# Two attention layers on one core: early queries with half the keys, and a new written order

## The chip, the cores and the metric

The kernel runs on one core of a Trainium2 chip. The metric is the device time of one execution in microseconds (us). A core has a matrix engine (TensorE, here PE; its weight loads are listed apart as PEld), a vector engine (VectorE, DVE), a scalar engine (ScalarE, ACT), a general engine (GpSimd, POOL) and a sync engine (SyncE, SP), which here only issues DMAs. Each engine works through its own queue in order and waits for others by semaphores. SBUF is the working memory with 128 partitions, PSUM the memory that PE writes.

## The reference, cut to what matters

There are 64 items of 128 positions with 512 features, and two attention layers one after the other. Both have 16 heads of 64 features, one key and one value shared by all heads, and one learned "null" key and value ahead of the 128 others. Each layer adds its normalised output to x.

```python
# one layer; q has 16 heads, k and v one
sim = einsum('bhid,bjd->bhij', q, k) + bias      # layer 1: * 8, q and k normalised
sim = where(causal, neg, sim)                    # key j hidden from query i if j > i
sim = where(mask, sim, neg)                      # padding of each item
attn = softmax(sim)                              # over the null key and 128 keys
out = einsum('bhij,bjd->bhid', attn, v)
return layernorm(out.reshape(b, n, 1024) @ Wo)
```

Layer 0 takes its bias from an input. Layer 1 makes it from the distance of two positions by a small network. Because of the causal mask, queries 0 to 63 see no key beyond 63.

## The kernel before, in words

**Tiling.** All of an item's 128 positions lie in the partitions. Matrix products with weights are done in three passes of float32r matmuls (high part by high, high by low, low by high), which `split_lo` (L125) and copies on ACT prepare. Layer 0 handles items in pairs: `Duo.direct` (L412) projects the first 14 heads of two items at once, already transposed; the last two heads come with key, value and null column from `Batch.project` (L535) and are transposed in `query_T` (L661). Layer 1 projects an item by `project` in three banks of 464, 448 and 256 columns (`BANKS`, L31), takes squared norms (`take`, L555; `power`, L581), scales (`scale`, L622) and transposes the queries in three parts.

**Softmax.** Four groups g of four heads follow. `bias_mask` (L683, POOL) adds bias and padding mask into a tile s of 128 x 4 x 129; five such tiles exist. `logits` (L697, PE) makes two pairs of heads: the stationary operand is two heads' transposed queries, the moving one a key tile of 256 columns (`kbh`, `kbl`) that holds the transposed key twice in block form, so one matmul gives two heads. `peak` (L706, DVE) adds and takes the maximum for each head; `exps` (L717, ACT) writes the null column and takes four exponentials with their sums; `recip` (L727, DVE) inverts the sums; `weigh` (L743, POOL) or, in layer 1 for groups 1 and 3, `weigh_scaled` (L734, ACT) multiplies.

**Transposition through DRAM.** `turn` (L753, DVE) transposes 32 x 32 blocks, `send` (L760) writes a group's blocks to DRAM, and `fetch` (L771) reads half an item (two groups h) back with the keys in the partitions, as `pT`. `values` (L778, PE) multiplies it with v in plain float32: two products of 64 output partitions each, side by side in the array. `values_high` (L790, ACT) and `values_low` (L794, DVE) split the result, `output` (L801, PE) does the three passes of the output projection per pair of heads. `out_stats` to `store` (L812 to L829) normalise, add and write.

**Order.** Nothing is scheduled by the compiler on PE, DVE, ACT and POOL: `STEPS` lists each step of a pair (layer 0) or an item (layer 1) with a time in units of `SPAN` (32.5 and 17.0 us), these are repeated for all pairs and items (`at`, L1106), sorted, and each engine's queue is filled in that order. The times are no clocks, only the order counts. SP is not in the list of ordered engines (`ENGINES`, L51). `OUT_STEPS` and `with_room` (L1122) put the preparation of later weights and of layer 1's bias in between; `begin` (L842) does the first pair's start by hand.

Of the kernel before, what the change touches and what calls it, by code (L numbers as in the profile page):

```python
# [28 lines left out]

# [3 lines left out]
    ((0, H + 7 * DH), (H + 7 * DH, 7 * DH), (H + 14 * DH, 4 * DH)),  # L33
# [3 lines left out]
VALC = (17 * DH, H + 7 * DH)  # L37
QHEADS = (((14, 16),), ((0, 6), (6, 12), (12, 16)))
QCOLS = (
    ((0, 16, 0),),  # L40
    ((0, 6, H + DH), (6, 10, H + 8 * DH)),
)
# [12 lines left out]
    mybir.EngineType.Pool,  # L55
}
# [3 lines left out]
def tile_two_attention_layers(ctx: ExitStack, tc: tile.TileContext, a, out: bass.AP):  # L60
# [24 lines left out]
    bias1 = pdr.tile([P, H, S], F32, tag="bias1", name="bias1")  # L85
# [137 lines left out]
    def by_column(t):  # L223

        return t.rearrange("p m (k b) -> p m b k", b=NS)

    def columns(t):
        return t.rearrange("p m (b k) -> p m b k", b=NS)

    def causal(bias, out):  # L230

        nc.gpsimd.affine_select(
            out=bias, in_=bias, compare_op=ALU.is_ge, fill=NEG, base=0,
            pattern=[[0, 4], [-1, S]], channel_multiplier=1,
        )
        nc.scalar.copy(columns(out), by_column(bias))

    def prep_bias1():
# [106 lines left out]
        def rows_of_table():  # L345

            work = p1.tile([P, 2, DIM], F32, tag="work", name="table")
            tb = work[0:H, 0, 0 : 2 * P]
            nc.vector.memset(tb, NEG)
            nc.vector.tensor_scalar_add(tb[:, S - 1 : 2 * S - 1], d["ps"], d["b2"])  # L350
            scratch = pdr.tile([H, 2 * P], F32, tag="scratch", name="scratch")
            nc.sync.dma_start(out=scratch, in_=tb)
            d["raw"] = wts.tile([P, H, S], F32, tag="wh1", name="raw_bias")
            nc.sync.dma_start(
                out=d["raw"],
                in_=bass.AP(scratch.tensor, scratch.offset, [[1, P], [2 * P, H], [1, S]]),
            )
            d["bias"] = wts.tile([P, H, S], F32, tag="wl1", name="bias1")

        def in_order(m):  # L360
            ms = slice(4 * m, 4 * m + 4)
            nc.scalar.copy(columns(d["bias"][:, ms, :]), by_column(d["raw"][:, ms, ::-1]))
            nc.sync.dma_start(out=bias1[:, ms, :], in_=d["bias"][:, ms, :])
# [17 lines left out]
    def mask_rows(L, b):  # L381
        if (L, b // MB) not in mu8s:
            mu8 = mu8s[L, b // MB] = p2.tile([P, MB, S], U8, tag="mu8", name="mu8")
            nc.sync.dma_start(
                out=mu8.rearrange("p b s -> p (b s)"),
                in_=masks[L].rearrange("b s -> (b s)")[b // MB * MB * S : (b // MB + 1) * MB * S]
                .partition_broadcast(P),
            )

    def mask_row(L, b):  # L390
        g = b // MB
        if (L, g) not in madds:
            madd = madds[L, g] = p2.tile([P, MB, S], F32, tag="madd", name="madd")
            nc.gpsimd.tensor_scalar(
                columns(madd), by_column(mu8s[L, g]), -NEG, NEG, ALU.mult, ALU.add
            )
        return madds[L, g][:, b % MB, :]

    class Duo:
# [34 lines left out]

        def direct_high(self, n):
            self.q[n] = [
                p1.tile([P, 2 - n // 3, 2, P], F32R, tag=f"qT{part}{n}", name="qT")
                for part in "hl"
            ]
            nc.scalar.copy(self.q[n][0], self.ps[n])  # L440

        def direct_low(self, n):
            split_lo(self.q[n][1], self.ps[n], self.q[n][0])

    class Batch:


        def __init__(self, L, b, t):
# [6 lines left out]
            self.q, self.qh, self.ql, self.pt_q = {}, {}, {}, {}  # L455
# [79 lines left out]
        def project(self, n, k, steps=None, columns=None):  # L535
# [4 lines left out]
            e = 4 if self.L == 0 else 2  # L540
# [14 lines left out]
        def take(self, n):  # L555
# [4 lines left out]
            if self.L == 0:  # L560
                self.q[n] = p1.tile([P, (h1 - h0) * DH], F32, tag="q0", name="q")
                nc.scalar.copy(self.q[n], ps[:, e : e + 2 * DH])
                return
            if n == 0:
                e = KEYC[1]
                self.rn = p4.tile([P, H + 1], F32, tag="rn", name="rn")
            m = (BANKS[1][n][1] - e) // DH
            rn = self.norms(n)
            for k in range(m):
                sq = p2.tile([P, DH], F32, tag="sq", name="sq")  # L570
                nc.scalar.activation(  # L571
                    sq, ps[:, e + k * DH : e + (k + 1) * DH], AF.Square,
                    accum_out=rn[:, k : k + 1],
# [18 lines left out]
        def value(self):  # L592

            self.v = p4.tile([P, DH], F32, tag="v", name="v")
            nc.vector.tensor_tensor(self.v, self.part(VALC, self.L, DH), nvrow, ALU.subtract)

# [12 lines left out]
        def null(self):  # L609

            self.nln, self.mx, self.den = (
                p4.tile([P, H], F32, tag=name, name=name) for name in ("nln", "mx", "den")
            )
            null = self.part(NULLC, 0, H)
            if self.L == 0:
                nc.vector.scalar_tensor_tensor(  # L616
                    self.nln, null, -1.0, self.w["nbias"], ALU.mult, ALU.subtract
                )
            else:
                nc.vector.tensor_scalar_mul(self.nln, null, -1.0)  # L620

        def scale(self, n):  # L622
# [5 lines left out]
            self.q[n] = p1.tile([P, nh * DH], F32, tag=("q0", "q1", "qTh3")[n], name="q")  # L628
            nc.vector.tensor_tensor(
                self.q[n].rearrange("p (h d) -> p h d", d=DH),  # L630
# [5 lines left out]
        def null_scale(self):  # L636

            nc.vector.tensor_tensor(self.nln, self.nln, self.rn[:, 1:], ALU.mult)  # L638
            nc.vector.tensor_tensor(self.nln, self.nln, self.w["nbias"], ALU.subtract)  # L639
# [4 lines left out]

        def key_high(self):
            self.kh, self.kl = kbh[self.t % NB], kbl[self.t % NB]
            for t in range(2):
                half = slice(t * DH, (t + 1) * DH)
                nc.scalar.copy(
                    columns(self.kh[half, t : t + 1, :]), by_column(self.pk[half, None, :])  # L650
                )

        def key_low(self):
            for t in range(2):
                half = slice(t * DH, (t + 1) * DH)
                split_lo(
                    columns(self.kl[half, t : t + 1, :]), by_column(self.pk[half, None, :]),
                    columns(self.kh[half, t : t + 1, :]),
                )

        def query_T(self, m):  # L661
            n = (QHEADS[self.L][m][1] - QHEADS[self.L][m][0]) // 2
            pt = self.pt_q[m] = ps_tr.tile([P, n, P], F32, tag="tr", name="pt_q")
            for k in range(n):
                nc.tensor.transpose(pt[:, k, :], self.q[m][:, k * P : (k + 1) * P], ident)  # L665

        def query_high(self, m):
            pt = self.pt_q[m]
            tag = f"qTh{m}" if self.L else "q1"
            self.qh[m] = p1.tile(list(pt.shape), F32R, tag=tag, name="qh")  # L670
            nc.scalar.copy(self.qh[m], pt)

        def query_low(self, m):
            pt = self.pt_q[m]
            tag = f"qTl{m}" if self.L else "ql"
            self.ql[m] = p1.tile(list(pt.shape), F32R, tag=tag, name="ql")
            split_lo(self.ql[m], pt, self.qh[m])
# [517 lines left out]
```

## Time and profile before

| what | value |
|---|---|
| time, median of 3 runs | 2434.31 us (2432.69 to 2436.56) |
| the profiled execution's own time | 2435.07 us |
| its span in the trace | 2433.2 us, granted PE clock 0.992 |
| PE busy | 2344.2 us (96%) |
| DVE busy | 2138.1 us (88%) |
| ACT busy | 1784.4 us (73%) |
| POOL busy | 1803.2 us (74%) |
| DMA | 455.72 MB, 62.3% of 16 engines' span |

The span reaches from the first to the last instruction; 1.9 us of the execution lie around it. In the views below, a row names line, engine, operation, what it writes from what it reads (out<-in), shapes and count; "idle" and "waited for" name the engine and line that ended a wait. Records of one engine overlap where its work is pipelined, so the distance of two starts tells more of a price than a record's length. In a timeline row the first column is the start and the second the length, in us.

### The profile page before, as it was taken

To read this page: it belongs to the slowest core of one execution; us is meant where nothing else is said; L and a number is where in the kernel's file an instruction comes from. 1 tells how busy PE (TensorE), PEld (TensorE's weight loads), DVE (VectorE), ACT (ScalarE), POOL (GpSimd) and SP (SyncE) were. 2 spreads that over 40 slices of the span, in tenths; PEclk is the share of its full clock that TensorE was granted. 3 is DMA by queue.
4 is the path that set the end of the run, shared out by engine and by line. 5 is a ranking of instruction groups with operands and counts; after the bars stand their busy time and mean duration, and the time that the engine had idled before them with its cause. 6 is when DMAs were issued, how large, how long until landed. Compare 5 with 4: busy or idle time off the path is not lost. (4 is left out here: it accounts for less than half of the span.)

```text
span 2433.2 us, 50606 instructions
## 1 busy us (share of the span) xinstructions
PE 2344.2 (96%) x13672; PEld 1870.6 (77%) x13672; DVE 2138.1 (88%) x7801; ACT 1784.4 (73%) x8424; POOL 1803.2 (74%) x2015
## 2 busy tenths in 40 slices
PE   5999999999999999999989999999999999999998
PEld 5778777778878878877677777778777777777785
DVE  7988888888888888888899999999999998999997
ACT  4656666656656656556578898899988898898985
POOL 5766677777776676676677888878877887888773
PEclk8999999999999999999999999999999999999999
DMA  5666666666666666666666666666666666666654
GB/s 171 188 175 202 200 198 185 195 207 193 198 202 183 192 192 184 192 191 186 202 188 175 193 180 193 189 182 195 184 188 182 183 190 183 175 192 190 181 170 143
DMA packets 568764, 455.72 MB, mean 187 GB/s; under 512 B 36112, under 2 KB 497952, under 8 KB 568480
## 3 DMA queue, kind: packets, MB, share of 16 engines
q1 hardware_dynamic: 568480, 452.50, 62.3%
q8 instruction: 109, 1.79, 0.3%
q14 instruction: 175, 1.43, 0.2%
HBM read 251.06 MB, written 201.34 MB: 186 GB/s over the span
## 5 line engine op out<-in xcount | busy, mean ns | idle before, releaser
L722 ACT ACTIVATE s<-s,mx 128x129 f32<-128x129 f32 x2048 | 800.4, 393 | 109.0 <-DVE mx L712 85.8
L685 POOL TENSOR_TENSOR s<-bias,madd 128x512 f32<-128x512 f32 x512 | 680.8, 1332 | 84.6 <-DVE den L729 68.2
L712 DVE CUSTOM_DVE_ANT_0 s<-sim,s,nln 128x128 f32<-128x128 f32 x2048 | 587.1, 344 | 1.9 <-PE sim L704 0.9
L747 POOL TENSOR_TENSOR s<-s,den 128x512 f32<-128x512 f32 x384 | 404.4, 1053 | 170.4 <-DVE den L729 102.6
L807 PE MATMUL y<-woh,oh 128*128 128x512 f32 x1024 | 416.3, 407 | 0.1
L807 PE MATMUL y<-wol,oh 128*128 128x512 f32 x1024 | 406.6, 397 | 0.7 <-DVE wol L127 0.7
L807 PE MATMUL y<-woh,ol 128*128 128x512 f32 x1024 | 404.0, 395 | 0.7 <-DVE ol L796 0.7
L755 DVE STREAM_TRANSPOSE tt<-s 128x512 f32<-128x512 f32 x512 | 353.8, 698 | 38.6 <-DMA turned<-tt 33.7
L722 ACT ACTIVATION_READ_ACCUMULATOR s<-s,mx 128x1 f32 x2048 | 382.5, 187 | 0.0
L546 PE MATMUL pq<-wh,xh 128*128 128x272 f32 (+3 forms) x1024 | 348.0, 340 | 2.5 <-DVE nln L638 2.3
L546 PE MATMUL pq<-wh,xl 128*128 128x272 f32 (+3 forms) x1024 | 344.2, 336 | 0.0
L546 PE MATMUL pq<-wl,xh 128*128 128x272 f32 (+3 forms) x1024 | 334.8, 327 | 0.0
L792 ACT ACTIVATE oh<-av,nvcol 128x512 fp32r<-128x512 f32 x256 | 174.8, 683 | 196.6 <-PE av L781 196.5
L781 PE MATMUL av<-pT,v 128*64 128x512 f32 x1024 | 277.5, 621 | 7.5 <-DMA pT<-turned 7.1
L107 POOL TENSOR_TENSOR rn<-rn,neghalf 128x7 f32<-128x7 f32 (+2 forms) x192 | 254.2, 1324 | 16.0
L428 PE MATMUL pqT<-xh,wh 128*128 128x256 f32 x896 | 255.1, 289 | 8.9 <-DVE nln L616 4.1
L428 PE MATMUL pqT<-xh,wl 128*128 128x256 f32 x896 | 253.3, 286 | 4.2 <-DVE wl L182 4.2
L428 PE MATMUL pqT<-xl,wh 128*128 128x256 f32 x896 | 254.3, 286 | 0.0
L571 ACT ACTIVATE sq<-pq 128x64 f32<-128x64 f32 x1088 | 225.6, 227 | 19.1 <-PE pq L546 17.4
L807 PEld LDWEIGHTS y<-woh,oh 128*128 128x128 f32 x1024 | 193.7, 189 | 53.8 <-issue 28.2
L807 PEld LDWEIGHTS y<-woh,ol 128*128 128x128 f32 x1024 | 193.3, 189 | 49.3 <-DVE ol L796 2.2
L546 PEld LDWEIGHTS pq<-wh,xh 128*128 128x128 f32 x1024 | 193.8, 189 | 48.4 <-issue 9.2
(106 smaller groups left out, 5831.9 us busy)
## 6 DMA issues: line engine op xcount, KB each, us to landing
turned<-tt SPq DMA_DIRECT2D x636, 256.0 KB, 3.5
pT<-turned SPq DMA_DIRECT2D x256, 512.0 KB, 4.3
xT<-turned SPq DMA_DIRECT2D x124, 256.0 KB, 3.1
x<-in_x_dram SPq DMA_DIRECT2D x64, 256.0 KB, 3.3
xr<-in_x_dram SPq DMA_DIRECT2D x64, 256.0 KB, 2.9
mid<-xr SPq DMA_DIRECT2D x64, 256.0 KB, 3.4
x<-mid SPq DMA_DIRECT2D x64, 256.0 KB, 3.7
xr<-mid SPq DMA_DIRECT2D x64, 256.0 KB, 2.8
```

The source lines that it names most:

```text
L107: nc.gpsimd.tensor_tensor(t, t, neghalf[:, 0:n], ALU.pow)
L428: nc.tensor.matmul(self.ps[n][:, hp, :, :], lhs[:, c, e : e + P], rhs[:, c, :, :],  start=(i == 0 and (hp == 0 or chunks is None)), stop=( ...
L546: nc.tensor.matmul(self.ps[n][:, c0:c1], lhs[:, c, :], rhs[:, c, n0 + c0 : n0 + c1], start=(i == 0), stop=(i == 3 * NC - 1),)
L571: nc.scalar.activation(sq, ps[:, e + k * DH : e + (k + 1) * DH], AF.Square, accum_out=rn[:, k : k + 1],)
L685: nc.gpsimd.tensor_tensor(s[:, :, 0:S], self.w["bias", g], self.mrow[:, None, :].to_broadcast([P, 4, S]), ALU.add,)
L712: nc.vector.tensor_tensor_reduce(s[:, k, 0:S], self.sim[g][:, k, :], s[:, k, 0:S], -1.0, self.nln[:, h : h + 1], ALU.add, ALU.min, self.mx ...
L722: nc.scalar.activation(s[:, k, :], s[:, k, :], AF.Exp, bias=self.mx[:, h : h + 1], scale=-1.0, accum_out=self.den[:, h : h + 1],)
L747: nc.gpsimd.tensor_tensor(s, s, self.den[:, gs, None].to_broadcast([P, 4, S]), ALU.mult)
L755: nc.vector.transpose(tt.rearrange("p b h i -> p h b i"), self.s[g][:, :, 0:S].rearrange("p h (b k) -> p h b k", k=SQ),)
L781: nc.tensor.matmul(av[t * DH : (t + 1) * DH], self.v, self.pT[h][:, :, t::2, :].rearrange("p i c q -> p c i q"), start=True, stop=True,)
L792: nc.scalar.activation(self.oh[h], self.av[h], AF.Identity, bias=nvcol)
L807: nc.tensor.matmul(self.y, lhs, rhs[:, c, :], start=(c == 0 and k == 0), stop=(c == NP - 1 and k == 2),)
```

## The change

The 64 early queries (f = 0) and the 64 late ones (f = 1) get tiles of their own. A query tile now has, in its 128 partitions after the logits, 64 queries of one head (m = 0) and the same 64 queries of another (m = 1); a group's row is 2 heads (t) by 64 + 128 keys (`KC` = 192), with a null column at each end: 2 x 194 in place of 4 x 129. The transposed query tiles are laid out accordingly.

- `logits`: per group three matmuls with 128 columns (early, 64 keys of two heads) and three with 256 (late), where six had 256.
- `peak`, `exps`, `weigh_scaled`: two operations over 64 keys and two over 128 where four had 128; `bias_mask`, `weigh` and `turn` 384 columns for 512; `recip` two instructions for one, because the late reciprocal is written twice for the broadcast.
- `null` and `null_scale` place the null columns by four operations on 64 partitions; `value` writes a second tile `ve`, the first 64 keys' values in the upper partitions.
- `send` once for half an item (384 KB) in place of twice (256 KB); `fetch` three transfers of 128 KB into `pTe`, the early tile that both halves share, and `pT`. Two of the `tt` tiles exist as before, now larger.
- `values(h)` only late queries (256 columns for 512); a new step `values_early` does both halves' early queries with 64 keys each, four products in 64 x 64 quarters of the array.
- Layer 1 projects in four banks (400, 256, 256, 256), with four `take`, `power`, `scale`, `query_T`, `query_high` and `query_low` for three.
- The bias of both layers, the causal mask and the padding mask are made in the new form; layer 0's bias comes by 16 loads in place of 4.
- All of `STEPS` and `OUT_STEPS` has new times, `START` of layer 1 is 11.58 us after the last pair's in place of 6.105, and SP joins the ordered engines.

```diff
-    ((0, H + 7 * DH), (H + 7 * DH, 7 * DH), (H + 14 * DH, 4 * DH)),
+    ((0, H + 6 * DH),) + tuple((H + (2 + 4 * n) * DH, 4 * DH) for n in range(1, 4)),
...
+HQ = S // 2
+KC = 3 * HQ
...
+    mybir.EngineType.SP,
...
         def logits(self, g):
-            sim = self.sim[g] = ps_sim.tile([P, 4, S], F32, tag="sim", name="sim")
-            for k in range(2):
-                qh, ql = self.query(2 * g + k)
-                o = sim[:, 2 * k : 2 * k + 2, :]
-                nc.tensor.matmul(o, qh, self.kh, start=True, stop=False)
-                nc.tensor.matmul(o, qh, self.kl, start=False, stop=False)
-                nc.tensor.matmul(o, ql, self.kh, start=False, stop=True)
+            sim = self.sim[g] = ps_sim.tile([P, 2 * KC], F32, tag="sim", name="sim")
+            for f in range(2):
+                qh, ql = self.query(g, f)
+                n = HQ * (f + 1)
+                kh, kl = (k[:, :, 0:n] for k in (self.kh, self.kl))
+                o = sim[:, f * S : f * S + 2 * n].rearrange("p (t k) -> p t k", t=2)
+                nc.tensor.matmul(o, qh, kh, start=True, stop=False)
+                nc.tensor.matmul(o, qh, kl, start=False, stop=False)
+                nc.tensor.matmul(o, ql, kh, start=False, stop=True)
...
         def recip(self, g):
-            den = self.den[:, 4 * g : 4 * g + 4]
-            nc.vector.reciprocal(den, den)
+            den, rd = self.den[:, g], self.rd[:, g]
+            nc.vector.reciprocal(rd[:, :, 0:1], den[:, :, 0:1])
+            nc.vector.reciprocal(rd[:, :, 1:3], den[:, :, 1:2].to_broadcast([P, 2, 2]))
...
         def fetch(self, h):
-            self.pT[h] = p1.tile([P, NS, 8, SQ], F32, tag=f"pT{h}", name="pT")
-            nc.sync.dma_start(
-                out=self.pT[h].rearrange("p i h q -> p i (h q)"),
-                in_=self.turned[h].rearrange("i p g n -> p i (g n)"),
-            )
+            if not self.pT:
+                self.pT["early"] = p1.tile([P, 4, 4 * SQ], F32, tag="pTe", name="pTe")
+            self.pT[h] = p1.tile([P, 4, 4 * SQ], F32, tag=f"pT{h}", name="pT")
+            early = self.pT["early"][h * HQ : (h + 1) * HQ]
+            for c, to in ((0, early), (1, self.pT[h][0:HQ]), (2, self.pT[h][HQ:S])):
+                nc.sync.dma_start(
+                    out=to,
+                    in_=self.turned[h][c].rearrange("(i k) b n -> (k b) i n", i=NS),
+                )
...
+        def values(self, h):
+            self.av[h] = ps_tr.tile([P, 4, 2, HQ], F32, tag="tr", name="av")
+            self.product(h, 1, self.v, self.pT[h])
+
+        def values_early(self):
+            for h, v in enumerate((self.v, self.ve)):
+                half = slice(h * HQ, (h + 1) * HQ)
+                self.product(h, 0, v[half], self.pT["early"][half])
...
-            (2.50268, 1, ("key_low",)),
-            (2.50918, 1, ("logits", 2)), (2.53737, 1, ("query_high", 0)),
+            (0.89797, 1, ("key_T",)), (0.90042, 1, ("value",)), (0.90738, 1, ("key_high",)),
+            (0.92340, 0, ("recip", 0)), (0.95978, 0, ("exps", 1)), (0.96346, 1, ("key_low",)),
+            (1.06758, 1, ("query_high", 0)), (1.09018, 1, ("logits", 0)),
+            (2.13455, 0, ("values", 0)), (2.14987, 0, ("values", 1)),
+            (2.16520, 0, ("values_early",)), (2.19690, 1, ("fetch", 0)),
+            (2.77385, 1, ("values", 0)), (2.78769, 0, ("values_low", 1)),
+            (2.82491, 1, ("values", 1)), (2.84024, 1, ("values_early",)),
...
+            (3.38051, ("fetch", 0)),
+            (3.68781, ("fetch", 1)), (3.98686, ("values", 0)), (4.01610, ("values", 1)),
+            (4.04535, ("values_early",)), (4.29385, ("values_high", 0)),
...
-    START = (0, B // 2 * SPAN[0] + 6.105)
+    START = (0, B // 2 * SPAN[0] + 11.58)
```

The helper that both value steps call is new:

```python
        def product(self, h, f, v, w):
            for t in range(2):
                nc.tensor.matmul(
                    self.av[h][t * DH : (t + 1) * DH, :, f, :], v,
                    w.rearrange("p (m i) (g t q) -> p t g m i q", m=2, t=2, q=SQ)[:, t]
                    .rearrange("p g m i q -> p g (m i) q"),
                    start=True, stop=True,
                )
```

## The prediction

> **What bounds the kernel now.** I read the page's engine totals first, then the same totals inside each layer, then the instruction starts on PE, then PE's waits.
>
> ```profile
> span 2433.2 us, 50606 instructions
> PE 2344.2 (96%) x13672; PEld 1870.6 (77%) x13672; DVE 2138.1 (88%) x7801; ACT 1784.4 (73%) x8424; POOL 1803.2 (74%) x2015
> ```
>
> ```profile
> core 0: us, PE busy (x) PEld busy (x) DVE busy (x) ACT busy (x) POOL busy (x), PEclk, DMA share, GB/s
> 300.00:1030.70 730.70, 711.85 (x4476) 577.10 (x4476) 620.24 (x2323) 444.41 (x1804) 523.00 (x548) 1.00 0.65 193
> 1380.00:2302.30 922.30, 912.82 (x5022) 719.71 (x5021) 850.36 (x3132) 820.04 (x4278) 743.68 (x869) 1.00 0.63 186
> ```
>
> The two stretches lie inside layer 0 (20 pairs of items) and layer 1 (50 items). PE is busy 97% and 99% of them at the full granted clock; DVE 85% and 92%, ACT 61% and 89%, POOL 72% and 81%. So PE sets the pace, and in layer 1 DVE is close behind. The pace itself is read from the starts of the residual addition, one per item:
>
> ```profile
> L825 DVE SCALAR_TENSOR_TENSOR xr<-yn,rs,xr x51: 707/719/748, 296.6 to 1210.0; 128x512 f32<-128x512 f32 x51
> L825 DVE SCALAR_TENSOR_TENSOR xr<-yn,rs,xr x52: 730/743/1856, 1353.1 to 2299.1; 128x512 f32<-128x512 f32 x52
> ```
>
> 913.4/50 = 18.27 us an item or 36.5 a pair in layer 0, 946.0/51 = 18.55 an item in layer 1. 32 x 36.5 + 64 x 18.55 = 2355; the other 78 us of the span are the start, the change of layers and the end.
>
> A busy share of matmuls is no measure of their price, because records overlap. The price is the distance between starts:
>
> ```profile
> 705.41 0.28 PE L428 MATMUL pqT<-xl,wh 128*128 128x256 f32 x1
> 705.53 0.28 PE L428 MATMUL pqT<-xh,wh 128*128 128x256 f32 x1
> 705.65 0.28 PE L428 MATMUL pqT<-xh,wl 128*128 128x256 f32 x1
> 705.86 1.08 PE L781 MATMUL av<-pT,v 128*64 128x512 f32 x4
> 706.87 0.39 PE L546 MATMUL pq<-wh,xh 128*128 128x272 f32 x1
> 707.09 0.29 PE L546 MATMUL pq<-wl,xh 128*128 128x272 f32 x1
> ```
>
> A float32r matmul with 256 columns takes 0.118 us (the mean of many; 512 columns 0.233 in the same way, in proportion). The values of half an item (four records: two halves of the output side by side, two passes) cost more than their 1.01: the first starts 0.21 after its predecessor instead of 0.12, and the matmul after next comes 0.22 after the next instead of 0.125. Together 1.01 + 0.09 + 0.10 = 1.2 us. With these prices a layer-0 pair is 84 x 0.118 + 24 x 0.126 + 48 x 0.118 + 48 x 0.233 + 4 x 1.2 + 4 transposes x 0.11 = 35.0 of its 36.5; a layer-1 item is 36 projections, 6.4, + 24 x 0.118 + 24 x 0.233 + 2 x 1.2 + 9 x 0.11 = 18.2 of 18.55. Stalls are thus 1.5 us a pair, 0.35 an item. Most of the former is one wait:
>
> ```profile
> 717.26 0.40 PE L807 MATMUL y<-woh,ol 128*128 128x512 f32 x1
> 717.74 0.35 PE L702 MATMUL sim<-kbh,qT 128*128 128x256 f32 x1
> 718.82 0.39 PE L703 MATMUL sim<-kbl,qT 128*128 128x256 f32 x1 [0.72 <-DVE kbl L127]
> ```
>
> The second logits matmul of an odd item waits for the low part of its key: from 717.26 to 718.82 is 1.56 where 0.233 + 0.118 would do, 1.2 us lost per pair.
>
> **The change, part by part.**
>
> *Logits, PE.* Per group three of six matmuls shrink from 256 to 128 columns: 12 an item, 1536 in all. The trace has no float32r matmul under 256 columns. In proportion one would take 0.06. But each brings its own weight load, and the nearest row with 128 columns and a load each is the query transpose:
>
> ```profile
> 1511.45 0.36 PE L546 MATMUL pq<-wl,xh 128*128 128x448 f32 x1
> 1511.65 0.38 PE L665 MATMUL pt_q<-ident,q 128*128 128x128 f32 x2
> 1511.79 0.45 PE L546 MATMUL pq<-wh,xl 128*128 128x448 f32 x1
> 1512.07 0.37 PE L546 MATMUL pq<-wh,xh 128*128 128x448 f32 x1
> ```
>
> From 1511.65 to 1512.07 two transposes and one 448-column matmul (0.204) pass: 0.108 a transpose. Here a rule speaks against the change: the Trainium skill, "TensorE: Matmul & The Clock Gate", section "LDWEIGHTS (loading the stationary operand)", says that a weight load takes its columns divided by 1.2 GHz, 107 ns for 128, however few columns then stream. The row fits that floor. By it the saving is 1536 x 0.010 = 15 us; by the same page's sustained 81 ns for a pair of load and 128-column matmul ("Back-to-back issue gap") it would be 57. I take 15, as the row is of this chip and this kernel. The dearest bound: a value pass streams 512 columns in 0.474, two passes 1.85 ns a column; should a short float32r matmul fall to that plain-float32 rate, 128 columns are 0.237 and the change costs 1536 x 0.119 = 183 us.
>
> *Values, PE.* Per item, before: 2 x 1.2 = 2.4. After: late queries, per half 256 instead of 512 columns, so half the streaming, 0.474; early queries of both halves once, four 64x64 quarters of the array. If they run side by side, another 0.474. Three groups x (0.474 + 0.06 of drain as now) = 1.6, plus the way in and out once if they stand together (0.19) and one change of tile shape between (0.1): 1.9, saving 0.5 an item, 64 us. The skill's "TensorEngine Tiling (Array Packing)", "Key Properties", warns that a change of tiling mode drains the array; the trace's price for that is the 0.09 + 0.10 above. In the new order the three steps stand together in layer 1 and for even items, apart for odd items: about 0.1 more for those, 3 us. If the two row halves do not overlap, the saving is 64 - 61 = 3 us.
>
> *Projection, PE.* Layer 1's 36 matmuls become 48 over the same 1168 columns; the twelve more cost about 3 ns each of fixed time. Nothing to speak of: 256 columns hide a weight load already now.
>
> *DVE.* Not the pace, but near it. Slope from the 384- and 256-column scalings (552 and 405 ns): 1.15 ns a column. Eight half-width peaks save 8 x 0.073 = 0.6 an item, four turns with 384 for 512 columns 0.6. Added: four more reciprocals at 0.09 (their distance to the next start), 0.35; three or four more null-column placements at 0.1, 0.35; the second value tile 0.2; in layer 1 a fourth scaling and low part, 0.2. Sum between -0.3 and 0: DVE stays at 31 a pair and 17.0 an item (850.36/50). It is hidden as long as PE is slower.
>
> *ACT and POOL.* Shorter exponentials, scalings and masks: at 0.93 ns a column ACT loses some 0.6 of layer 1's 16.4; POOL at 2.2 ns a column loses 1.1 on masks and 0.6 to 1.1 on weighing, and gets 0.8 back in layer 1 from four norm roots for three. Both lie under PE; worth nothing by themselves.
>
> *Transfers and SP.* Per item four sends of 256 KB and two fetches of 512 become two of 384 and six of 128; issues go from six to eight at some 0.4 to 0.55 us each, about 3 us of SP's time as before. SP is now in the written order too: behind a waiting send stand loads of later items. In the written times a fetch stands at least 5.6 us ahead of its values in both layers, against 4.3 us to landing now; it is hidden, with 1.3 us to spare. If it were late, PE's values and DVE's low halves behind them would be.
>
> *Order.* The key's low part now stands at 0.963 of a pair and its logits at 1.090: 4.1 us apart (0.2 before), so the 1.2 us go. But both engines are near full and their queues strict, so some new wait will show; I book 0.6 a pair, and 0.15 an item in layer 1, for it. At the ends: twelve more small bias loads ahead of the output weights, and layer 1's written start is 5.5 us later, so the two layers' ends have to be packed anew: I take +10, bounds -20 and +40.
>
> *Sum.* Layer 0: -12 x 2 x 0.010 - 2 x 0.5 - 1.2 + 0.6 = -1.85 a pair, 32 of them -59. Layer 1: -0.12 - 0.5 + 0.15 = -0.47, 64 of them -30. Ends +10. Together -79 against the profiled execution: 2435 - 79 = 2356. The median of the runs is 0.8 below the profiled one: **2355 us**.
>
> **Rivals.**
> 1. *Short float32r matmuls are slow* (the other side). Place: the three early logits matmuls. Price up to 0.237 each: 2355 + 15 + 183 = 2553. It decides from 79/1.536 = 51 ns above the 0.108 taken, that is 0.16 us, on. For: nothing in the trace runs that type under 256 columns, and plain float32 takes two passes. Against: from 256 to 512 columns the price is straight with almost no fixed part.
> 2. *The new order stalls.* The 1.2 us only move and layer 1 stalls as layer 0 does now (1.5/36.5, 4%, 0.75 for 0.35): 2355 + 19 + 38 = 2412, somewhat more if the change of layers suffers. For: DVE at 92% and PE at 99% leave no slack. Against: PE is the slowest, which gives the others some.
> 3. *DVE becomes the bound in layer 1.* 17.0 at its present 92% gives 18.5 for 18.1: +26, 2381. For: its work doesn't fall. Against: it had 8% idle because it waited for PE.
> 4. *Early values do not overlap*: +61, 2416.
>
> **How the numbers follow.** Main case 0.48 (own range 2315 to 2400), rival 1 0.20, rival 2 0.15 (a third of it slower than before), rival 3 0.10, rival 4 0.07. A measurement of this kernel tells 0.2% (5 us) from no change. Faster: 0.48 + 0.10 + 0.07 + 0.07 = 0.72; same: 0.03; slower: 0.20 + 0.05 = 0.25. For 8 in 10 the range covers everything but rival 1's dear end and a rest below: 2305 to 2490.
>
> **What would show it.** Right: 128-column logits start 0.105 to 0.11 apart; values_early's four outputs start within some 0.02 and the next matmul follows 0.5 us after; the wait on the key's low part is gone; residuals come 34.6 a pair and 18.1 an item apart. Wrong: early logits 0.2 or more apart (rival 1); PE's share in layer 1 under 96% with waits on DVE (2 and 3); a values group of early queries of 1 us (4). The prediction falls with any of these, or if the ends lose more than 40 us.

## The result and the profile after

The changed kernel takes 2446.14 us (median of 10 runs, 2441.45 to 2456.81), the kernel before 2435.26 beside it (10 runs, 2423.15 to 2437.88): ratio 1.0053, 95% interval 1.0034 to 1.0071. It is slower by 0.5%, where 2355 us and a gain were forecast. The profiled execution took 2445.07 us. The head of its page, and the same two stretches as before by engine:

```profile
span 2443.3 us, 56032 instructions
PE 2300.5 (94%) x15464; PEld 1936.2 (79%) x15464; DVE 2186.7 (89%) x8953; ACT 1697.1 (69%) x8492; POOL 1635.7 (67%) x2141
```

```profile
core 0: us, PE busy (x) PEld busy (x) DVE busy (x) ACT busy (x) POOL busy (x), PEclk, DMA share, GB/s
300.00:1030.70 730.70, 710.59 (x4913) 601.88 (x4912) 638.21 (x2713) 424.79 (x1841) 455.12 (x558) 0.99 0.58 171
1380.00:2302.30 922.30, 893.26 (x5972) 748.67 (x5970) 888.06 (x3610) 781.83 (x4303) 703.91 (x965) 1.00 0.53 157
```

In layer 1 PE fell from 99% to 97% of the stretch, and DVE rose from 92% to 96%. The residual additions, one an item:

```profile
L929 DVE SCALAR_TENSOR_TENSOR xr<-yn,rs,xr x52: 709/750/1517, 304.5 to 1233.3; 128x512 f32<-128x512 f32 x52
L929 DVE SCALAR_TENSOR_TENSOR xr<-yn,rs,xr x52: 739/761/1560, 1351.5 to 2304.3; 128x512 f32<-128x512 f32 x52
```

Layer 1 has 952.8/51 = 18.68 us an item (18.55 before; 18.08 forecast). In layer 0 I count from the 11th to the 51st residual, 20 whole pairs: 35.65 us a pair (36.57 before; 34.65 forecast). The ten residuals after that are left out, since there PE already makes 144 projection matmuls of layer 1, where the kernel before makes 18. What the matmuls themselves cost is as forecast. Layer 0 on PE, one group of logits, a key's transpose and then the values of an item:

```profile
711.51 0.22 PE L786 MATMUL sim<-kbh,qT 128*128 128x128 f32 x1
711.57 0.28 PE L787 MATMUL sim<-kbl,qT 128*128 128x128 f32 x1
711.68 0.27 PE L788 MATMUL sim<-kbh,qT 128*128 128x128 f32 x1
711.79 0.34 PE L786 MATMUL sim<-kbh,qT 128*128 128x256 f32 x1
711.97 0.28 PE L787 MATMUL sim<-kbl,qT 128*128 128x256 f32 x1
712.08 0.28 PE L788 MATMUL sim<-kbh,qT 128*128 128x256 f32 x1
712.20 0.27 PE L714 MATMUL pt_k<-ident,kd 128*128 128x128 f32 x1
712.40 0.65 PE L873 MATMUL av<-pT,v 128*64 128x256 f32 x4
713.58 0.65 PE L873 MATMUL av<-pT,v 128*64 128x256 f32 x4 [0.52 <-DMA pT<-turned]
714.16 0.43 PE L873 MATMUL av<-pTe,v 64*64 64x256 f32 x2
714.17 0.43 PE L873 MATMUL av<-pTe,ve 64*64 64x256 f32 x2
714.43 0.38 PE L873 MATMUL av<-pTe,v 64*64 64x256 f32 x2
714.44 0.38 PE L873 MATMUL av<-pTe,ve 64*64 64x256 f32 x2
```

The second and third 128-column matmul take 0.11 us to the next start, the first 0.06, and the 256-column one behind them 0.18 in place of 0.118. A group takes 0.69 us; six matmuls of 256 columns took 0.71. The early values' quarters start 0.01 apart, so both row halves run at once; a late group takes 0.58. So rivals 1 and 4 are out. But the second late group waits here for its softmax weights, and the first comes to 1.18 us instead of 0.58. In this stretch of layer 0 the kernel before had no such wait.

In layer 1, from the 71st to the 121st residual (50 items), PE waited for this (total, times, longest):

```profile
PE pq L601 <- DVE ve L653: 17.8, 24, 1.1
PE y L911 <- DVE yn L924: 5.0, 24, 0.2
PE av L873 <- DMA pT<-turned: 3.9, 8, 1.6
```

The third projection bank waits for the second value tile, every other item; the output's first matmul waits for the norm of the item before. The view lists idle time between two records only: a matmul can come later than it could without a gap between them. My first theory (A) took these two waits by their word.

### The profile page after: what moved, and what is told of

It reads as the page before. It is cut to its first block, busy times and chain, and to the rows that moved or that the text cites. A ratio compares the mean times of both kernels' runs of the same rounds, so it can differ in the third digit from the quotient of the medians.

```text
span 2443.3 us, 56032 instructions
## 1 busy us (share of the span) xinstructions
PE 2300.5 (94%) x15464; PEld 1936.2 (79%) x15464; DVE 2186.7 (89%) x8953; ACT 1697.1 (69%) x8492; POOL 1635.7 (67%) x2141
## 4 chain that ended last, share of the span: by engine, by line
DVE 38%; PE 36%; DMA 14%; issue 5%; SPq 3%; POOL 2%; ACT 1%; DVEq 0%; POOLq 0%; ACTq 0%
PE y L911 11%; PE pqT L470 11%; DVE s L798 7%; DMA turned<-tt 6%; PE pq L601 4%; PE av L873 4%; DVE tt L843 4%; DMA pT<-turned 3%; DVE qT L129 3%; DVE q L700 3%; DVE tt L549 3%; DVE ol L898 2%; DVE xr L929 2%; DMA xr<-in_x_dram 2%; DVE st L114 2%
## 5 line engine op out<-in xcount | busy, mean ns | idle before, releaser
L768 POOL TENSOR_TENSOR s<-bias,madd 128x384 f32<-128x384 f32 x512 | 570.7, 1130 | 295.3 <-DVE tt L843 252.4
L809 ACT ACTIVATE s<-s,mx 128x65 f32<-128x65 f32 (+1 forms) x2048 | 745.4, 366 | 16.7
L798 DVE CUSTOM_DVE_ANT_0 s<-sim,s,nln 128x64 f32<-128x64 f32 (+1 forms) x2048 | 517.4, 311 | 48.2 <-PE sim L788 41.6
L601 PE MATMUL pq<-wh,xh 128*128 128x256 f32 (+2 forms) x1280 | 390.4, 305 | 25.8 <-DVE ve L653 25.8
L833 POOL TENSOR_TENSOR s<-s,rd 128x384 f32<-128x384 f32 x384 | 322.4, 843 | 130.9 <-DVE rd L818 130.9
L601 PE MATMUL pq<-wl,xh 128*128 128x256 f32 (+2 forms) x1280 | 381.8, 298 | 0.0
L601 PE MATMUL pq<-wh,xl 128*128 128x256 f32 (+2 forms) x1280 | 381.3, 298 | 0.0
L843 DVE STREAM_TRANSPOSE tt<-s 128x384 f32<-128x384 f32 x512 | 280.7, 563 | 49.7 <-DMA turned<-tt 37.8
L786 PE MATMUL sim<-kbh,qT 128*128 128x128 f32 (+1 forms) x1024 | 297.9, 291 | 23.7 <-DVE mx L798 20.3
L788 PE MATMUL sim<-kbh,qT 128*128 128x128 f32 (+1 forms) x1024 | 286.5, 280 | 8.6 <-DVE qT L129 8.5
L787 PE MATMUL sim<-kbl,qT 128*128 128x128 f32 (+1 forms) x1024 | 287.1, 280 | 1.8 <-DVE kbl L129 1.5
```

The lines of the kernel that those rows point to most:

```text
L601: nc.tensor.matmul(self.ps[n][:, c0:c1], lhs[:, c, :], rhs[:, c, n0 + c0 : n0 + c1], start=(i == 0), stop=(i == 3 * NC - 1),)
L768: nc.gpsimd.tensor_tensor(s[:, :, 1 : KC + 1], self.w["bias", g], self.mrow[:, None, :].to_broadcast([P, 2, KC]), ALU.add,)
L786: nc.tensor.matmul(o, qh, kh, start=True, stop=False)
L787: nc.tensor.matmul(o, qh, kl, start=False, stop=False)
L788: nc.tensor.matmul(o, ql, kh, start=False, stop=True)
L798: nc.vector.tensor_tensor_reduce(s, sim, s, -1.0, self.nln[:, g, t, f : f + 1], ALU.add, ALU.min, self.mx[:, g, t, f : f + 1],)
```

## The experiments

Each set is given as a ratio to the kernel before, run beside it on the same chip; that kernel's own median was 2422.6 in the first set, 2427.8 in the second, 2442.1 in the third. Across sets, ratios can be compared, device times cannot. Some recorded expectations take the changed kernel's pace in layer 1 as 18.3 us an item; counted from the 71st to the 121st residual it is 18.62.

### First set: the two waits, the order, the tiles, SP

**e1_value** and **e2_value_turn**: the value ahead of the residual on DVE; then the transpose of x behind the output's norm as well.

```diff
-            (0.06843, ("scale", 0)), (0.12455, ("value",)), (0.15460, ("project", 2, 0)),
+            (0.06843, ("scale", 0)), (0.07500, ("value",)), (0.15460, ("project", 2, 0)),
```

```diff
-            (-2.78081, ("norm",)), (-2.50980, ("turn_x",)), (-2.23794, ("send_x",)),
+            (-2.78081, ("norm",)), (-2.35400, ("turn_x",)), (-2.23794, ("send_x",)),
```

> The changed kernel, with layer 1's value step (the two value tiles) written at 0.075 of an item instead of 0.12455, so ahead of the residual on DVE. Theory A (layer 1 loses its time to two waits of PE on DVE, of which the wait of the third projection bank for the second value tile is 0.43 us an item): 64 x 0.43 = 27 us less than the changed kernel, about 2419 us, ratio to before 0.993, residuals in layer 1 17.9 us apart instead of 18.3. Theory B (DVE is simply full, the wait only moves to the output's first matmul or another place): 2440 to 2446, residuals 18.2 to 18.3 apart.

> As e1_value, and layer 1's turn of x (1 us of DVE) is written behind out_norm instead of ahead of out_stats, so that the one bank of the output comes free earlier. Theory A: the second wait (output's first matmul for out_norm, 0.32 us an item) goes too: 64 x 0.75 = 48 us less than the changed kernel, about 2398 us, ratio 0.985, residuals 17.55 apart. Theory B (DVE full): no more than 10 us below the changed kernel, 2436 or more, DVE busy over 95% of layer 1.

Measured: 2481.33 us, ratio 1.0231 (1.0207 to 1.0255), and 2489.09, 1.0259 (1.0235 to 1.0283). Both are slower than the changed kernel by 2%; both theories missed. The wait for `ve` is gone, and others are longer. In e1_value, over the same 50 items, DVE's longest wait and then PE's two:

```profile
DVE tt L843 <- DMA turned<-tt: 32.9, 23, 3.1
```

```profile
PE y L911 <- DVE yn L924: 24.6, 46, 0.6
PE av L873 <- DMA pT<-turned: 17.4, 17, 2.3
```

DVE's next transposed tile waits until an earlier one has been sent, PE for softmax weights that are fetched late. The wait that theory A named was cured, and DVE and the transfers behind it got later. What PE waits for was a symptom.

**e3_old_tiles**: the new order with the old softmax and value tiles. The step lists, starts, the four query banks and SP's place are those of the changed kernel, the functions below those of the kernel before; sends go with each `turn`, `values_early` is empty. One more thing differs from the kernel before: three tiles `tt` exist for transposed blocks, where it and the changed kernel have two.

```diff
         def logits(self, g):
-            sim = self.sim[g] = ps_sim.tile([P, 2 * KC], F32, tag="sim", name="sim")
+            sim = self.sim[g] = ps_sim.tile([P, 4, S], F32, tag="sim", name="sim")
...
         def values_early(self):
-            for h, v in enumerate((self.v, self.ve)):
-                half = slice(h * HQ, (h + 1) * HQ)
-                self.product(h, 0, v[half], self.pT["early"][half])
+            pass
```

> The new order of all instructions (step times, start of layer 1, room for preparations, SP in the written order, four query banks in layer 1) with the old tiles: 128 keys for all queries, four heads of 128 queries in a group, values of half an item at once, no second value tile. PE's work is then the 2275 us of the kernel before. Theory A (the new order makes the stalls): PE time without work stays near the changed kernel's 217 us less the 27 us of the second value tile, time 2465 to 2490, layer 1 residuals 18.6 to 19 apart, start and change of layers as late as in the changed kernel. Theory C (the new tiles make the stalls by more and smaller instructions on DVE and SP): time within 10 us of the kernel before, 2425 to 2445, stalls about 150 to 170.

Measured: 2483.51 us, 1.0246 (1.0220 to 1.0272): as theory A had it for the order. The new order costs the old tiles 2.5%; the new tiles, in the ordered form, give 1.9% of it back. That PE's stalls were the changed kernel's less the second value tile's didn't hold in the parts: layer 1 takes 18.87 an item, more than the changed kernel, without any wait for `ve`.

**e4_sp_free**: SP isn't held to the written order; the order on the four other engines is the changed kernel's to the last instruction.

```diff
-    mybir.EngineType.SP,
```

> The changed kernel with SP taken out of the written order, so that SP's issues are ordered by the scheduler as before. Theory D (waiting sends at the head of SP's queue delay loads and fetches at the start and in the change of layers): first residual at 125 us or earlier instead of 145.7, change of layers (residuals 60 to 64) some 10 us shorter, time 2420 to 2430. Rival: SP is hidden, nothing changes by more than 0.3%, 2439 to 2453.

Measured: 2379.97 us, 0.9815 (0.9797 to 0.9833), three times theory D's gain and not where D put it: the first residual moves only from 145.7 to 141.1 us. Layer 0 runs at 34.96 us a pair for 35.65, layer 1 at 17.96 an item for 18.62. The same two stretches:

```profile
core 0: us, PE busy (x) PEld busy (x) DVE busy (x) ACT busy (x) POOL busy (x), PEclk, DMA share, GB/s
300.00:1030.70 730.70, 719.40 (x5028) 615.43 (x5025) 664.82 (x2774) 435.03 (x1891) 464.08 (x567) 1.00 0.56 173
1380.00:2302.30 922.30, 917.26 (x6200) 776.50 (x6199) 903.32 (x3734) 810.99 (x4457) 733.02 (x998) 1.00 0.52 162
```

What SP held up in layer 0 is seen in the changed kernel's waits (20 pairs, 332 to 1045 us), SP's own and PE's:

```profile
SPq L567 <- POOL xl L584: 107.5, 20, 7.1
SPq L865 <- PE av L873: 97.9, 39, 4.0
```

```profile
PE av L873 <- DMA pT<-turned: 9.4, 10, 1.7
```

Once a pair SP stands 5.4 us before a fetch of x, until POOL frees the one buffer for it, and twice 2.5 us until PE frees the buffers of the softmax weights; sends and other fetches stand behind. In e4_sp_free PE has no such wait for weights in those 20 pairs, nor has DVE one for a sent tile in layer 1.

### Second set: is it the tiles' transfers, the place of one step, or DVE?

By now the waits of e1 pointed to DVE. Its instructions in layer 1 don't have one duration. The changed kernel's DVE and POOL, one item and the next:

```profile
1708.81 1.33 DVE L536 TENSOR_SCALAR x<-x,mv,rs 128x512 f32<-128x512 f32 x1
1708.85 1.01 POOL L768 TENSOR_TENSOR s<-bias,madd 128x384 f32<-128x384 f32 x1 [0.87 <-DVE rd L817]
1710.07 0.16 DVE L709 TENSOR_TENSOR nl<-nl,rn 128x16 f32<-128x16 f32 x1
...
1725.96 2.25 POOL L768 TENSOR_TENSOR s<-bias,madd 128x384 f32<-128x384 f32 x2
...
1726.82 0.52 DVE L536 TENSOR_SCALAR x<-x,mv,rs 128x512 f32<-128x512 f32 x1
1727.25 1.00 DVE L709 TENSOR_TENSOR nl<-nl,rn 128x16 f32<-128x16 f32 x1
```

The normalisation of x takes 0.52 us or 1.33, a multiplication of 16 columns 0.16 or 1.00. Each long one ends only after POOL's addition of bias and mask, beside which it ran (1708.85 to 1709.86, and the second of the two in the row from 1725.96, which ends at 1728.21). The Trainium skill ("SBUF — State Buffer", section "SBUF: two separate sides") has the rule: DVE and GpSimd share a pair of SBUF ports as an exclusive lock, which a DVE instruction with two SBUF inputs (against a GpSimd one that reads SBUF) or in a 2-port mode needs; the second to come is blocked until the first is through. The multiplication, with two SBUF inputs, agrees. For the normalisation no run here shows which mode it is in, and the order isn't the page's: its long record begins 0.04 us ahead of POOL's, and it is the one held.

So theory E: in the changed kernel DVE sets layer 1's pace, and what it loses beside POOL counts. For every kernel I took the pace over those 50 items and subtracted what three kinds of instructions take beyond their undisturbed time (x over 0.517, the residual over 0.740, the null columns over 0.163 us) and DVE's waits. The rest is DVE's own work. That the columns add up to the pace is so by construction, for any engine, and proves nothing. What speaks for the theory is that DVE hardly waits for anything but a sent tile (0.02 to 0.15 us an item in every kernel with the new tiles, except e1 and e2 with 0.2), while its own work stays between 17.12 and 17.28 us (e13 apart, which adds to it):

| kernel | ratio to before | pace, us an item | lost to POOL | DVE waits for a sent tile | DVE's other waits | rest: own work | idle PE between records, waiting for DVE |
|---|---|---|---|---|---|---|---|
| before | 1 | 18.53 | 0.41 | 0.28 | 0.96 | 16.88 | 0.12 |
| changed | 1.0053 | 18.62 | 1.06 | 0.29 | 0.08 | 17.19 | 0.46 |
| e1_value | 1.0231 | 19.37 | 1.29 | 0.66 | 0.17 | 17.25 | 0.54 |
| e2_value_turn | 1.0259 | 19.40 | 1.27 | 0.64 | 0.21 | 17.28 | 0.58 |
| e3_old_tiles | 1.0246 | 18.87 | 1.89 | 0 | 0.01 | 16.98 | 0.46 |
| e4_sp_free | 0.9815 | 17.96 | 0.83 | 0 | 0.02 | 17.12 | 0 |
| e6_old_tiles_sp_free | 1.0092 | 18.86 | 1.89 | 0 | 0 | 16.97 | 0.46 |
| e7_value_sp_free | 0.9955 | 18.66 | 1.39 | 0 | 0.04 | 17.22 | 0.52 |
| e8_null | 0.9707 | 17.60 | 0.34 | 0 | 0.08 | 17.18 | 0 |
| e9_store | 1.0087 | 18.75 | 1.01 | 0.44 | 0.09 | 17.21 | 0.44 |
| e10_null_sp | 1.0115 | 19.16 | 1.12 | 0.70 | 0.15 | 17.19 | 0.78 |
| e11_start | 0.9652 | 17.59 | 0.33 | 0 | 0.09 | 17.18 | 0 |
| e12_before_dve | 1.0248 | 19.79 | 1.82 | 0.25 | 0.51 | 17.21 | 0.59 |
| e13_after_dve | 1.0076 | 18.77 | 0.98 | 0.18 | 0.06 | 17.55 | 0.42 |

**e6_old_tiles_sp_free**: e3_old_tiles with the line of e4_sp_free.

> The new order with the old tiles (as e3_old_tiles), and SP taken out of the written order (as e4_sp_free). Theory D (the written order of SP's issues makes the stalls, whatever the tiles): as much is gained from e3_old_tiles as the changed kernel gained, 2.4% of the kernel before: ratio 0.995 to 1.002, PE time without work about 135 to 145 us. The tiles are then worth the distance to e4_sp_free, 0.015 to 0.02. Rival (it is the new tiles' more and smaller transfers that a written order of SP holds up): less than half of it, ratio 1.012 or more.

Measured: 2452.90 us, 1.0092 (1.0069 to 1.0116), between the two forecasts. Layer 0 gains as with the new tiles: its 61st residual comes at 1224.1 us for 1253.2, 29 us earlier (changed kernel to e4_sp_free: 1233.3 to 1200.9, 32). Layer 1 gains nothing, 18.86 for 18.87: in both, POOL costs DVE 1.89 us an item and no tile is waited for, with three tiles `tt` to fill. So SP's order hurts layer 0 with either tiles, and layer 1 has a further cause. Whether a third `tt` tile would have spared the changed kernel its waits was not tried. With SP free, the new tiles are worth the distance from here to e4_sp_free, 1.0092 to 0.9815: 2.8%.

**e7_value_sp_free**: e1_value with the line of e4_sp_free.

> As e1_value (the value tiles ahead of the residual in layer 1), with SP taken out of the written order. In e1_value DVE's instructions are 0.23 us an item longer than in the changed kernel (they meet POOL's mask additions) and DVE waits 0.45 us an item more for a transposed tile to be sent. Theory D (these come from SP's order, and from the shift against POOL that it makes): within 0.4% of e4_sp_free, ratio 0.978 to 0.986. Rival (the value's place does the harm by itself): ratio 0.990 or more.

Measured: 2419.42 us, 0.9955 (0.9939 to 0.9972), as the rival had it. The 0.66 us of waits for sent tiles are gone with SP's order, but 1.39 us are lost to POOL where e4_sp_free loses 0.83: with the value earlier, the residual and x both meet one of POOL's additions in every item.

**e8_null**: e4_sp_free, and one step moved.

```diff
-            (1.21458, ("bias_mask", 0)), (1.25004, ("null_scale",)), (1.45227, ("logits", 0)),
+            (1.21458, ("bias_mask", 0)), (1.32000, ("null_scale",)), (1.45227, ("logits", 0)),
```

> e4_sp_free, and layer 1's null_scale written at 1.32 of an item, between two peaks, instead of 1.25. In e4_sp_free its first multiplication of 16 columns takes 0.955 us in the mean where it takes 0.16 when POOL isn't adding a bias and a mask from two SBUF tiles at the time. Theory E (layer 1 is now held by DVE, whose time per item is its work plus what it loses to POOL): that falls to about 0.2, DVE has 0.8 us an item less, and PE's 0.34 us of stalls an item become the limit of the gain: 10 to 20 us, ratio 0.973 to 0.977, residuals 17.4 to 17.55 apart. Rival (PE sets the pace of layer 1, DVE is covered): ratio 0.980 to 0.983, residuals 17.7 apart.

Measured: 2359.37 us, 0.9707 (0.9687 to 0.9728): theory E, and a little more than it forecast. The multiplication in e4_sp_free and in e8_null (busy, mean ns, idle before):

```profile
L708 DVE TENSOR_TENSOR nl<-nl,rn 128x16 f32<-128x16 f32 x51 | 47.0, 922 | 0.0
```

```profile
L708 DVE TENSOR_TENSOR nl<-nl,rn 128x16 f32<-128x16 f32 x51 | 8.8, 173 | 0.0
```

It takes 0.75 us less; x is held in 19 items of 49 instead (0.32 an item), and the pace falls by 0.36 to 17.60. On PE the gain is seen where the output's first matmul needs the norm that DVE makes, first in e4_sp_free, then in e8_null:

```profile
PEld y L910 <- DVE yn L923: 21.3, 49, 0.5
1906.30 0.35 PE L600 MATMUL pq<-wh,xl 128*128 128x400 f32 x1
1906.75 0.50 PE L910 MATMUL y<-woh,oh 128*128 128x512 f32 x1
1907.09 0.39 PE L910 MATMUL y<-wol,oh 128*128 128x512 f32 x1
```

```profile
1910.67 0.35 PE L600 MATMUL pq<-wh,xl 128*128 128x400 f32 x1
1910.86 0.39 PE L910 MATMUL y<-woh,oh 128*128 128x512 f32 x1
1911.09 0.39 PE L910 MATMUL y<-wol,oh 128*128 128x512 f32 x1
```

The two distances are 0.44 and 0.34 us in the mean of the 50 items of e4_sp_free, and 0.19 and 0.23 in e8_null: 0.36 less, the whole gain. So DVE held PE in e4_sp_free too, though the table's last column shows nothing there: the weight load waits (the first row), under the record of the matmul before. In e8_null neither PE nor this weight load waits for DVE. In the changed kernel the two distances are 0.50 and 0.34, 0.41 too many; with the two other waits shown above, for `ve` and for `pT` (17.8 and 3.9 us in 50 items), that is 0.84 of the 1.02 us by which its item is longer than e8_null's.

**e9_store**: the changed kernel, one SP step moved.

```diff
-            (5.61408, ("out_root",)), (6.08685, ("residual",)), (6.13273, ("store",)),
+            (5.61408, ("out_root",)), (6.08685, ("residual",)), (6.30000, ("store",)),
```

> The changed kernel, SP still in the written order, with one step moved: layer 1's store of the result at 6.30 of an item instead of 6.13, so behind the two sends of the weights and the reload, not ahead of them. Theory D, in its narrow form (the store, waiting 8.9 us an item at the head of SP's queue for the residual, holds the sends behind it, and DVE's next transpose waits for them 0.3 us an item and drifts against POOL): layer 1 gains 0.3 to 0.6 us an item, 20 to 35 us, ratio 0.991 to 0.997. Rival (many places of SP's order together, this one alone does little): ratio 1.002 to 1.007.

Measured: 2450.86 us, 1.0087 (1.0061 to 1.0112): no gain, and DVE waits 0.44 us an item for sent tiles. So layer 1's store is not what costs the time, though it stands longest at the head of SP's queue. That SP has nothing else to do then would fit, and was not tested.

### Third set: the reverse tests, and the start

**e10_null_sp**: the changed kernel with e8's step.

> The changed kernel, SP still in the written order, with layer 1's null_scale alone moved to 1.32 as in e8_null. Theory E (DVE holds layer 1 in the changed kernel too: 16.9 us of its own work an item, 1.07 that three of its instructions lose while POOL adds bias and mask, 0.36 of waits for a sent tile, against a pace of 18.30): the 0.41 us of the null columns goes, 64 x 0.41 = 26 us, ratio 0.993 to 0.998; and wherever the time ends, 16.9 plus the loss to POOL plus DVE's waits must give the pace within 0.1 us. Rival (SP's order alone sets layer 1): ratio 1.003 to 1.008.

Measured: 2471.46 us, 1.0115 (1.0099 to 1.0130), slower than either forecast. The multiplication is short (0.17), but the placements behind it meet POOL now (0.52 us an item), and the waits for sent tiles rise from 0.29 to 0.70. DVE's own work is again 17.19; the sum tells where the time went, but not beforehand where the phases fall.

**e12_before_dve** and **e13_after_dve**: in the kernel before and in the changed one, two more subtractions in layer 1's value step (the lines as in e13_after_dve).

```diff
+            if self.L == 1:
+                for _ in range(2):
+                    more = p1.tile([P, DH], F32, tag="more", name="more")
+                    nc.vector.tensor_tensor(more, v, nvrow, ALU.subtract)
```

> The kernel before, with two more subtractions of 64 columns on DVE in layer 1's value step, 0.44 us an item, whose result nothing uses[...]. Theory E (before, PE set layer 1's pace and DVE waited 1.2 us an item): hidden, ratio 0.999 to 1.004. Rival (DVE set the pace there too): 64 x 0.44 = 28 us, ratio 1.010 to 1.013.

> The changed kernel with the same two more subtractions on DVE in layer 1. Theory E (DVE sets the pace of layer 1): 28 us more, ratio to before 1.013 to 1.020. Rival (PE or SP sets it): within 0.4% of the changed kernel, 1.003 to 1.009.

Measured: 2505.89 us, 1.0248 (1.0230 to 1.0266), and 2462.12, 1.0076 (1.0059 to 1.0094). Theory E's forecasts fail for both, in opposite directions: the kernel before loses far more than even its rival had, and the changed kernel lies where the rival had it (PE or SP sets the pace). 0.44 us of records, 0.33 in the table's own work, cost the kernel before 1.26 us an item. In it the residual was held in 5 items of 50 and the multiplication of the null columns in 23; in e12_before_dve in 50 and 49. First the kernel before, then e12_before_dve (1420 to 2330 us):

```profile
L825 DVE SCALAR_TENSOR_TENSOR xr<-yn,rs,xr 128x512 f32<-128x512 f32 x49 | 39.3, 803 | 0.0
L638 DVE TENSOR_TENSOR nln<-nln,rn 128x16 f32<-128x16 f32 x49 | 18.9, 386 | 0.0
```

```profile
L829 DVE SCALAR_TENSOR_TENSOR xr<-yn,rs,xr 128x512 f32<-128x512 f32 x46 | 72.1, 1568 | 0.0
L642 DVE TENSOR_TENSOR nln<-nln,rn 128x16 f32<-128x16 f32 x46 | 38.6, 839 | 0.0
```

The loss to POOL rises from 0.41 to 1.82 us an item. DVE's other waits fall only from 0.96 to 0.51, so DVE is not full here; PE's idle time before a query's low part rises instead (28 us in 50 items, 6 before). The two engines wait for each other, and how that multiplies the loss was not taken apart. The changed kernel takes the same two instructions for 0.15 us: its own work rises by 0.36, the loss falls by 0.08 and the waits by 0.13. So e13 by itself doesn't decide for theory E; the nearly gapless DVE and e8_null do. A shift of 0.4 us changed the loss to POOL by -0.1 to +1.4 us, by what it met.

**e11_start**: e8_null with four weight halves later at the start.

```diff
-            (-492.48, "low", 7), (-473.73, "low", 2), (-137.5, "low", 0), (-61.66, "low", 1),
+            (58.0, "low", 7), (62.0, "low", 2), (66.0, "low", 0), (70.0, "low", 1),
```

> e8_null, and four of the low halves of layer 0's output weights are written at 58 to 70 us instead of ahead of everything. At the start PE stands 15.8 us, from 37.4 on, for the first peaks, and DVE stands 3.9 us of them for the casts of those weights and then works 2.5 us on them. If these 6.4 us are on the path: 6 us less, ratio 0.967 to 0.969. Rival (the bias and mask additions of POOL, which end at 54 us, hold the peaks as well): 0 to 2 us, ratio 0.970 to 0.971.

Measured: 2359.02 us, 0.9652 (0.9637 to 0.9667), the lowest ratio and below both forecasts, but the kernel before was 0.6% slower on that chip than in the second set, and the device time is e8_null's. The spans of the profiled executions are 2353.9 us for e8_null's 2357.0, so some 3 us of the 6 came. PE's stand falls only by 2.3 us, from 15.76 to

```profile
51.32 0.45 PE L785 MATMUL sim<-kbh,qT 128*128 128x128 f32 x1 [13.42 <-DVE mx L797]
```

since DVE, no longer waiting for the weights' casts, now waits for an input. SP issues that load at 34.37 us, after the 16 bias loads that it issues from 21.64 to 33.07 us:

```profile
42.20 0.69 DVE L113 BATCH_NORM_STATS2 st<-x 128x6 f32<-128x512 f32 x1 [3.23 <-DMA x<-in_x_dram]
```

In its two stretches PE is busy 98.4% and 99.9%:

```profile
300.00:1030.70 730.70, 719.12 (x5025) 614.89 (x5024) 666.67 (x2770) 434.66 (x1891) 462.70 (x567) 1.00 0.56 173
1380.00:2302.30 922.30, 921.80 (x6330) 797.96 (x6329) 896.54 (x3818) 822.41 (x4550) 739.79 (x1011) 1.00 0.52 164
```

## Why the prediction was wrong

The miss is 89 us (2445 profiled against 2356). By the stretches: layer 0, 35.65 for 34.65 a pair, 32 x 1.00 = 32; layer 1, 18.62 for 18.08 an item, 64 x 0.54 = 35; the ends, 2443.3 - 32 x 35.65 - 64 x 18.62 = 111 against 78 before, +33 for +10. Two steps of the prediction failed, *Transfers and SP* and *DVE*; the sum of PE's own work did not.

**The sum of PE's work was right.** Without stalls it was forecast as 35.0 - 0.24 - 1.0 = 33.8 us a pair, and 18.2 - 0.12 - 0.5 = 17.6 an item. e4_sp_free runs at 34.07 a pair between its 31st and 51st residual, e8_null at 17.60 an item with no wait of PE for DVE. *Logits*: about 0.11 us for a load and a 128-column matmul stands in the trace, as the row and the Trainium skill's rule for the weight load had it, not the 0.081 of the other section. *Values*: the halves overlap. *Projection*: no trace of a cost. The key's wait went as said.

**Transfers and SP failed.** The step saw SP's strict order, booked it as hidden with 1.3 us to spare, and named who would wait if not. It compared written times of one fetch with its landing and didn't ask what each issue waits for at the head of the queue. PE's values did wait. Taking the order away gives 0.69 us a pair, 22 of layer 0's 32 us; e6 shows the same with the old tiles. The other 10 lie in the pairs from the 11th to the 21st residual, where even e4_sp_free takes 37.40 us. Layer 1's weights and bias are prepared there; that this is the cause was not tested. I booked 0.6 a pair over all. Which of SP's issues it is in layer 0 was not separated; e9_store moved only one of layer 1's.

**DVE failed, and with it the cover of layer 1.** The step had DVE's work fall by up to 0.3 us an item and hid it under PE. Its own work rose by 0.3 (16.88 to 17.19 in the table). In part its terms were too small: placing the null columns takes four operations with a mean of 0.17 us in e8_null where the sum had 0.1 each. And the duration taken, 17.0, contained losses to POOL as if they were work. Those went from 0.41 to 1.06 us in the new order, the waits for sent tiles stayed at 0.29, and the slack (0.96 of other waits) was gone. 17.19 + 1.06 + 0.29 + 0.08 = 18.62. This is rival 3 with more than its price: it put 17.0 at a 92% share, without a cause for the share. Rival 2, stalls of the new order, named the kind, but not where they come from. *Order* booked 0.15 for layer 1; the measured excess over PE's 17.6 is 1.0. The sign set for rivals 2 and 3, PE's share of layer 1 under 96%, just failed to show (97%), though the waits on DVE were there.

That SP's order also sets part of layer 1's loss is shown by e4_sp_free (0.29 to 0 of waits, 1.06 to 0.83 lost to POOL); that the loss to POOL alone is on the path, by e8_null. SP's written order in the kernel before, by itself, was not tried.

**The ends** stayed inside their bounds (+33 of at most +40), but the booked 10 was too low. The first residual comes at 145.7 us for 108.8, while the last seven items take 83 us for 94. PE's stand for the first peaks grew from 9.7 to 15.6 us; e11_start moved it by 2.3. The rest was not taken apart.

## What to carry to other kernels

When two engines are near full, take from the trace the shortest time of each instruction beside its mean. Where the same form takes two durations, look for what runs beside the longer one: such a collision moves when anything in the order moves. Before a DMA queue is put into a written order, list for each issue what it waits for and which issues are behind it; a queue that only "has room" can still hold everything. And a stall that ends last on the busiest engine tells where the lateness arrives, not where it arises: e1_value and e2_value_turn removed two such stalls and lost 2%.

## What the runs showed of the hardware beyond that

Two more DVE instructions of 0.22 us each cost 1.26 us an item (e12_before_dve), while two others then met POOL in nearly every item: the residual, beside POOL's low part of x (0.80 to 1.57 us in the mean), and the null columns, beside an addition of bias and mask (0.39 to 0.84). POOL is held too: in the changed kernel an addition that begins inside an undisturbed x or residual takes 1.23 us or more, one that begins clear of them 0.99 to 1.03. Not every POOL instruction blocks: in the changed kernel the residual at 1724.39 us took 0.74 while POOL's power of a few columns, which also reads SBUF, was running. Nor is every DVE instruction held: a subtraction that reads PSUM kept its 0.22 us beside an addition (`v` at 1725.05). And of a run of three 128-column matmuls the first came cheap (0.06 us to the next start), while the longer one behind them paid 0.06 more.
